# A planned order with corrected costs, and constant products ahead of planned TensorE waits

## The chip, the cores and the metric

The kernel runs on one core of one Trainium2 chip. A core has engines that run side by side: TensorE (PE; its weight loads are listed as PEld), VectorE (DVE), ScalarE (ACT), GpSimd (POOL) and SyncE (SP), which here issues nearly all DMA transfers. The metric is the device time of one launch in microseconds (us), lower is better. A profile is one execution recorded by the hardware profiler.

## The reference, cut to what matters

The input is 32 images of 56 x 56 pixels with 96 channels. Each goes through a conditional convolution block, a frequency-domain mixing layer and a quantised feed-forward layer:

```python
pooled = mean(x, (1, 2)); rw = sigmoid(pooled @ Wr + br)            # 4 expert weights per image
h = relu(bn1(x @ sum_e rw[e] * Wpw[e] + rw @ bpw))                   # 96 -> 384
h = relu(bn2(sum_e rw[e] * (depthwise3x3(h, Wdw[e]) + bdw[e])))
x = bn3(h @ sum_e rw[e] * Wpwl[e] + rw @ bpwl) + x                   # 384 -> 96

t = tokens(x)                                                        # 3136 x 96
h = relu(bn(layernorm(t) @ w1.T))                                    # 96 -> 192
X = fft(h, over tokens); xr, xi = relu(complex diagonal of X + bias)
t = t + bn(real(ifft(xr + 1j * xi)) @ w2.T)                          # 192 -> 96
u = relu(q(q8(layernorm(t)) @ q8(W1).T + b1))                        # 96 -> 384, q8: float8 e5m2
t = t + q(q8(u) @ q8(W2).T + b2)                                     # 384 -> 96, q: float16
```

## The kernel before, in words

After a preparation (constants, the transform matrices, the first image's loads) the whole run is recorded as a list of operations, image by image, by `record(b)` (line 767). Nothing is issued while it is recorded. An operation (`Op`, line 151) is one small piece of work on one engine: a group of matmuls, one copy out of PSUM, one DMA. It has a planned duration, a due time, the buffers that it reads, writes and takes, and a function that emits its instructions.

`Plan.order()` (line 269) then plays the list through as a small event simulation. Each engine starts, among the operations whose inputs are done and whose buffers are free, the one with the earliest due time. The due time is set from the table `WANT` (when in the image's period a stage should run), plus `NUDGE`, one number per operation of an image (572 of them, sought beforehand by an automatic search), minus `HURRY` for the DVE and ACT operations that read PSUM, so that they go first. An operation's input counts as ready after a lag per engine, and for a DMA after its modelled landing (`DMA_LAG`, `packets`), plus the reader's `slack`: 2.0 us for a DMA that `move` (line 231) records, unless it is given, and none for `add` (line 236). Buffers come from rings; PSUM is one ring of eight banks (`Banks`, line 97), from which an operation takes one, two or four when it starts, and to which they are given back when the last reader is done. At the end (lines 1477 and 1478) the operations are emitted in the order in which the simulation started them, and `Pinned` (line 370) keeps that order in the program. On the chip, each engine works its instructions off in this order; semaphores make it wait where an operand or a place is not there yet.

The stages of an image, with the names that the profile shows:

- `pad` (line 787, ACT) copies the loaded image into a padded layout and sums it; `spread` and a small matmul (`ps<-wr_s,pooled`) give the four expert weights; `mixed` (line 831, DVE) mixes the weights.
- The expansion (`ps<-x,wk`). Of six groups of 128 channels, three get their depthwise convolution from VectorE (`by_vector`, 869) and three from TensorE (`by_tensor`, 928): DMAs regroup the channels (`hp<-h`), `conv` (line 976) runs 128 small matmuls `ps<-hp,wg`, and DMAs bring the result back (`h<-hp`). `project` (1030) is `ps<-h,wk` and `ps<-h,wkc`.
- `moments` (1075) transposes strips of the image (`ps<-ident,x`) and takes their mean and variance, with a power function on POOL (`root`); `hidden` is `ps<-w1c,x`; `along_h` (1161) is the transform along h (`ps<-ha,da`), stored to DRAM as gd.
- The frequency stage, in seven groups of four or five frequencies: a load `g2`, `along_q` (1215, `ps<-dftb_s,g`; its first group also has `ps<-ones,nsa`), element-wise work on ACT and DVE (tiles za, zb, tmpa, tmpb), `second` (1288, `ps<-w2b,zb` and `ps<-w2a,za`), `back_q` (`ps<-zo,dftc_s`), stored to DRAM as yd.
- The last stage, in four strips: loads `yt`, `dd`, `xs`; `back_h` (1361, `ps<-dd,yt`) transforms back, DVE adds into xs, `moments` again (`ps<-ident,xs`), `normal` on ACT, `turn_back` (1397, `ps<-ident,nt`), `up` (1416, `ps<-n,fw`, three times), ReLU on ACT, a cast on POOL, `down` (1442, `ps<-h,fw`, three times), the addition on POOL and the store. The tile `h16` between `up` and the cast has two places.

Operations of up to three images are under way at once, so that one image's last stage runs beside the next one's convolutions.

Of the kernel before, what the change touches and what calls it, by code (L numbers as in the profile page):

```python
# [18 lines left out]
NE = 4  # L19
C = 96  # L20
M = 384
# [7 lines left out]
PB = 2 * S  # L29
# [48 lines left out]
class Ring:  # L78


    def __init__(self, places):
        self.places = places
        self.rest = 0.0
        self.free = list(range(len(places)))
# [8 lines left out]
    def give(self, got):  # L93
        self.free.extend(got)

# [55 lines left out]
class Op:  # L151
    __slots__ = ("eng", "dur", "due", "emit", "bufs", "takes", "left", "ready", "after", "end", "seq", "size", "slack", "port")
# [12 lines left out]
def packets(n, size):  # L165
# [7 lines left out]
WANT = dict(period=113.9, half=60.1, expand=0.0, vector=1.4, forward=10.7, forward_step=27.0, freq=172.2,  # L173
            freq_step=7.0, tail=259.2, tail_step=26.5, x=17.0, mix=33.5, project=33.0)

HURRY = 666.0
# [6 lines left out]
    -172.8, -9.2, -163.5, -60.3, 106.2, -144.5, 5.2, 53.2, -138.8, -8.2, -18.1, 99.5, 147.5, 94.2, 30.4, 67.4, 92.4, -148.5,  # L183
    -6.5, -38.5, 17.2, -12.9, -15.4, -66.7, 8, 47.3, 43.1, -21, 54, 5.1, 79, 62.9, 70.9, 46, 65.8, 61.6,
    84.4, 85, 84.4, 40.6, -2.1, 87.1, 20.9, 22, 0.2, 78.2, 60.5, 28.6, 19, 81.3, 37.6, 57.2, 88.1, 56.4,
    66.3, 27.8, 87.7, 47.1, 3.9, -118.2, -64.2, -84.3, -87, 1.7, 38, -13.3, 3.3, 79.4, -68.9, 6.1, -39.3, -22.4,
    -19.6, 33.1, 71.9, 22.4, 90.3, 8.3, 105.6, -2.6, 53.5, -90.3, -62.6, -103.8, -44.5, 28.1, 84, 81.8, 41.1, 65.4,
    8.5, -38.6, -23.9, -6.9, 6.4, 31.1, 20.5, -24.2, -49.9, -25.7, -1.2, 35.9, 4.4, 29.3, 35.4, 31.7, 11.2, 32.7,
    -0.6, 2.9, 64.3, 55.4, 21.5, 6, 26.4, -13.2, -2.6, -11, -7.5, -46.8, -15.5, -65, -6.8, -1.4, -9.5, -61.2,
    -31.8, -58.5, 20.3, 11.2, -20.3, -4.1, -1.5, -38.9, -22.4, 22.3, 23.7, -10.1, 25.5, 18, -0.4, 34.1, 24.9, 15.9,  # L190
    16.3, -10.2, 31.4, 20, 22.3, 21.4, 68.6, 6.5, 20.6, 32.1, 45.3, 0.2, 87.8, 97.5, 26.2, 165.3, 25.8, 69.2,
    -2.3, 75.7, -13.1, 128.9, -49.1, -108.2, -48.2, -13.1, 8.1, -3, 25.2, 64.8, 93.3, -26.5, -18, -36.1, -44, 25,
    40.1, 17.9, -68.7, -67.4, -63.8, -83.2, 48.6, -63, 51.9, -62.9, 51.9, 52.1, -44.3, -24.4, -95.9, 11.6, 10.1, -125.8,
    -87.7, -2.9, -83.3, 1.2, -12.6, -52.9, -15.4, 74.6, -82.7, 30.3, -7, 42.3, 39.1, -114.4, 9.2, -95.3, 27.5, 21,
    -15.1, 18.2, 13.7, -47.5, 10, 15.9, -62.4, -63.7, 18.7, -75.9, 1.4, -102.1, 66, 13.6, -89.4, -47.9, -79.5, 7.9,
    27.8, -78.8, -48.7, -13.9, -80.9, 7.2, -17, -75.7, 2.9, 34.7, -79.6, 18.7, -29.5, -51.1, 29.1, -120.2, -27, -174.8,
    -19.6, -1.7, -101.7, -132.1, -25.7, -135.5, -3.1, -29.4, -68.3, -35, -106.8, -36.1, -32.9, -24.2, -19.8, -72.9, -51.2, -26.6,
    -193.3, -161, -26, -32.5, -13, -23, 2, -38.4, -26.7, -48.1, -139.2, -94.1, -29.8, -21.3, -65.4, -22.5, -55.3, -54.9,
    -104, 2.6, 50, -62.3, -1.2, -99.1, -50, -31.3, -93.3, -124, -30.2, 30.5, -6.3, -48.4, 9.1, -63.1, 23.9, -32.4,
    -123.4, -98.1, -13.4, -29.5, 2.9, -15.5, -54.1, -85.5, -81.5, -70, -65.3, -64.4, -9.9, -63.4, -67.9, -49.2, -238.5, -138.2,  # L200
    -51.4, -18.7, -39.4, -87.4, -30.3, -73.9, -33.3, -80.2, -229.8, -126.4, -52, -64, -103.4, -40.4, -65.3, -50.3, -83.5, -2.5,
    -2.7, -75.9, -43, -126.9, -9.5, -24.2, -129.6, -23.3, 4.8, 37.3, 44.5, 14.3, 64.3, -80.5, 24.6, -6, -141, -113.4,
    -0.5, -18.6, 6.6, -17.9, -90.6, -142.3, -89.1, -9.7, 39.2, 0.3, 64.2, -29.5, 14.3, 27.4, -160.3, -34.4, 20.7, 9.1,
    18.6, 19.1, 34, -87.3, 22.2, -20.8, -79.3, -114.3, -21, -1.7, -46.5, 1.5, -56.6, -68.3, -96, -11.4, 7.3, -31,
    -1, -113.3, -20.1, -2.5, -133.2, -104.9, -6.8, 32.5, -0.9, 15.3, 67.8, -62.8, 32.2, -0.4, -84, -89.1, 48.2, -11,
    9.3, 43.2, -1.5, -48, -40.4, 3.9, 40.7, -28.9, 46.7, -47.5, 12.9, 24.6, -140.4, -106.2, 23.3, 13.5, -12.4, 27.8,
    13.9, -47.3, -7.4, 5.3, -87, -93, 11.7, 18.1, -83.2, -13.4, -87, -74.7, 14.1, 53.6, 39.4, 15.6, -33.3, 7,
    -90, -14.5, -32.6, -58, -68.1, -127.6, 70.6, -91.1, -82, -120.2, -128, -95.6, -46.5, -198.2, -126.4, -74.2, -83.7, -138.5,
    -99, -84.9, -60.2, -28.1, 23.8, -92.6, 27.3, -29.5, -3, 14.7, 11.8, 22.6, 27.2, -37.4, -126.3, -32, -88.4, -49.7,
    -80.9, -115.3, 44.8, -36.2, -64.3, -126.9, -78.2, -25.2, -36.4, -46, -79, -23.3, -32.1, -93.1, -97.6, -15.3, -44.1, 7.2,  # L210
    69.9, -69, -43.9, 51.1, 2.7, 75.7, 49.8, 54.4, 62.2, -32.2, -53.4, 7.7, -51.1, -6.4, 24.5, -84.8, 136.4, -14.6,
    6.6, -88.3, -65, 0.9, -18.3, -70.5, -45.5, 2.6, -12.9, -65.1, -65.4, -0.1, -18.6, -23.2, 77.8, -37.1, 0.8, -7.6,
    5, 67.2, 25.4, 103.6, 150.3, 33.5, -55.5, 40.7, -47.9, 2.3, 49.7, -3.5, 176, 13.2, -18.2, -66.6, -65.7, -28.6,
    15.8, -58.1, 11, 16.7, -29, -88, -20.9, 33.5, -35.4, 17.5, 44.4, -13.1, 48.4, 59.1,
# [4 lines left out]
class Plan:  # L219
# [16 lines left out]
    def add(self, eng, dur, due, emit, reads=(), writes=(), takes=(), size=0, port=None):  # L236
        op = Op()
# [5 lines left out]
        op.takes, op.size, op.slack = list(takes), size, 0.0  # L243
# [25 lines left out]
    def order(self):  # L269
# [19 lines left out]
        def start(op, now):  # L289
            for b in op.takes:  # L290
                b.got = b.ring.take(b.n)
            begin = now
# [41 lines left out]
        while events:  # L334
            now = events[0][0]
            while events and events[0][0] <= now:
# [11 lines left out]
                elif kind == "give":  # L348
                    for b in x.bufs:
                        b.users -= 1  # L350
                        if b.users == 0:
                            if b.ring.rest:
                                push(now + b.ring.rest, "back", b)
                            else:
                                b.ring.give(b.got)
                else:
                    x.ring.give(x.got)
# [28 lines left out]
def kernel(  # L386
# [380 lines left out]
    def record(b):  # L767
# [7 lines left out]
        for st in range(NS):  # L775
# [11 lines left out]
            def pad(st=st, h=h, k=k, sx=sx):  # L787
# [8 lines left out]
                takes=[mix, *xh] if st == 0 else [],  # L796
# [39 lines left out]
        def mix_wk2():  # L836
# [8 lines left out]
            "DVE", 3.08, t0 - WANT["mix"], lambda: mixed(wk.ap, wpw_s, wpw_s[:, NE], C + 1), port=True,  # L845
# [82 lines left out]
        def by_tensor(h, c, due, hid):  # L928
# [47 lines left out]
            def conv():  # L976
# [13 lines left out]
                "PE", 3.8, due, conv, reads=[(wg, 0), *((hp, r) for r in range(4))],  # L990
# [84 lines left out]
        def moments(p, of, key, due, out_extra):  # L1075
# [30 lines left out]
            add("POOL", 1.78, due + 1, root, port=False, writes=[(ln, 0)])  # L1106
# [3 lines left out]
        for st in range(NS):  # L1110
# [22 lines left out]
            for q0, nq in ((0, 4), (4, 3)):  # L1133
# [27 lines left out]
                def along_h(q0=q0, nq=nq, ps=ps, ha=ha, da=da):  # L1161
# [11 lines left out]
                    "PE", 0.82, due + 3, along_h, reads=[(ha, 0), (da, 0)], writes=[(ps, 0)], takes=[ps, g],  # L1173
# [24 lines left out]
        for i, (k0, nk) in enumerate(GROUPS):  # L1198
# [7 lines left out]
                reads=gd_parts, writes=[(g2, 0)], takes=[g2],  # L1206
# [268 lines left out]
    for b in range(NB):  # L1475
        record(b)
    for op in plan.order():
        op.emit()
# [114 lines left out]
```

## Time and profile before

| what | value |
|---|---|
| median of 3 runs | 4395.16 us (4389.32 to 4395.35) |
| profiled execution, its own time | 4390.8 us |
| its span, first to last instruction | 4389.0 us |
| mean granted TensorE clock | 0.95 |
| TensorE busy | 3988.9 us (91%) in 40066 matmuls |
| VectorE, ScalarE, GpSimd busy | 3551.2, 3110.9 and 1632.2 us |
| DMA | 679.25 MB, mean 155 GB/s |
| chain of work that ended last | PE 46%, ACT 19%, DVE 13%, DMA 9%, POOL 6% |

A line of the profile names the engine, the operation, what it writes and reads by the program's tile names without their numbers, the shapes, and a count. Where every operation goes through one helper, all have that helper's line (L380), so one reads by names. In brackets or behind the last bar stands the time that the engine stood idle before the instruction, and what ended it; where several operands were awaited, the one that came last by the profile is named. "issue" means that nothing in the profile was awaited. A busy time of PE is the union of its matmuls from start to modelled end.

### The profile page before, as it was taken

What the parts mean: (1) busy time and instruction counts of PE and PEld (TensorE: products, weight loads), DVE (VectorE), ACT (ScalarE), POOL (GpSimd) and SP (SyncE); (2) the same over time, 40 slices, a digit from 0 to 9 for tenths busy, and PEclk for the clock granted to TensorE, in tenths of its full rate; (3) what the DMA queues carried; (4) which work ended last, traced back from release to release, by engine and by line L of the source; (5) the groups of instructions that cost most, each with busy time, mean ns of one, the idle gap of its engine ahead of it and who ended that gap; (6) DMA issues with size and microseconds to landing.
All of it is one profiled execution on the core that took longest, in us unless ns stands there. A gap on an engine that the chain in (4) does not pass through costs nothing.

```text
span 4389.0 us, 104599 instructions
## 1 busy us (share of the span) xinstructions
PE 3988.9 (91%) x40066; PEld 2522.6 (57%) x40066; DVE 3551.2 (81%) x9036; ACT 3110.9 (71%) x6281; POOL 1632.2 (37%) x1332
## 2 busy tenths in 40 slices
PE   2888999999999999999999999999999999999985
PEld 0455655666565665655666655566565566665663
DVE  5877777798888889877888888888977888888853
ACT  1456766677777777766778777777876777877765
POOL 1223333333334434333333434433433333343333
PEclk9988999999999999999999999999999999999986
DMA  5754776666776666676666777666667666667642
GB/s 119 139 140 118 168 162 144 154 147 170 172 169 164 162 161 160 164 160 149 154 154 154 174 175 168 167 161 152 162 162 162 159 156 149 162 170 178 157 130 65
DMA packets 427749, 679.25 MB, mean 155 GB/s; under 512 B 155062, under 2 KB 290678, under 8 KB 427206
## 3 DMA queue, kind: packets, MB, share of 16 engines
q1 hardware_dynamic: 421632, 668.08, 64.8%
q8 instruction: 316, 5.18, 0.5%
q10 hardware_dynamic: 5618, 4.49, 0.4%
q14 instruction: 183, 1.50, 0.1%
HBM read 300.21 MB, written 211.04 MB: 116 GB/s over the span
## 4 chain that ended last, share of the span: by engine, by line
PE 46%; ACT 19%; DVE 13%; DMA 9%; POOL 6%; issue 4%; SPq 1%; POOLq 0%; ACTq 0%; DVEq 0%
PE ps L380 46%; ACT h L380 6%; ACT nt L380 5%; POOL ln L380 5%; DVE ln L380 3%; DVE ha L380 3%; ACT tmpa L380 2%; DMA hp<-h 2%; DMA yt<-yd 2%; DMA da<-dad 2%; DVE za L380 2%; DVE tmpa L380 2%; DVE h L380 1%; ACT tmpb L380 1%; ACT y L380 1%
## 5 line engine op out<-in xcount | busy, mean ns | idle before, releaser
L380 DVE SCALAR_TENSOR_TENSOR h<-h,small,h 128x784 f32<-128x784 f32 x1536 | 1557.0, 1050 | 103.3 <-ACT h L380 84.5
L380 POOL CAST h<-h 128x784 fp8e5<-128x784 f16 x384 | 511.2, 1335 | 738.3 <-ACT h L380 738.3
L380 PE MATMUL ps<-x,wk 97*32 97x435 f32 (+2 forms) x3840 | 698.7, 571 | 9.3 <-DVE wk L380 9.1
L380 POOL TENSOR_TENSOR ln<-ln,mhalf 120x7 f32<-120x7 f32 (+1 forms) x256 | 473.9, 1851 | 21.3
L380 PE MATMUL ps<-hp,wg 32*32 32x392 f32 x12288 | 420.4, 520 | 48.6 <-DMA hp<-h 28.1
L380 POOL TENSOR_SCALAR ln<-ln 120x7 f32<-120x7 f32 (+1 forms) x256 | 130.0, 508 | 866.4 <-DVE ln L380 866.4
L380 PE MATMUL ps<-dftb_s,g 112*128 112x112 f32 (+1 forms) x3776 | 432.1, 288 | 12.5 <-DVE tmpa L380 9.9
L380 ACT ACTIVATE h<-ps 128x435 f32<-128x435 f32 (+2 forms) x768 | 388.7, 543 | 69.8 <-PE ps L380 55.6
L380 PEld LDWEIGHTS ps<-dftb_s,g 112*128 112x128 f32 (+1 forms) x3776 | 353.3, 172 | 143.9 <-issue 41.9
L380 DVE SCALAR_TENSOR_TENSOR ha<-ps,ln,nshift 120x192 f32<-120x192 f32 x896 | 306.4, 408 | 155.7 <-PE ps L380 150.3
L380 DVE BATCH_NORM_STATS2 ln<-ps 120x6 f32<-120x96 f32 (+1 forms) x1792 | 315.8, 247 | 69.2 <-PE ps L380 68.5
L380 PEld LDWEIGHTS ps<-x,wk 97*32 97x32 f32 (+1 forms) x3840 | 203.6, 125 | 276.1 <-issue 141.9
L380 ACT ACTIVATE h<-h,fb 128x784 f16<-128x784 f16 x384 | 361.1, 965 | 1.3
L380 PEld LDWEIGHTS ps<-hp,wg 32*32 32x32 f32 x12288 | 218.7, 105 | 232.0 <-issue 106.9
L380 PE MATMUL ps<-w1c,x 96*120 96x192 f32 x1792 | 342.7, 342 | 6.6 <-issue 5.5
L380 ACT ACTIVATE nt<-ps,ln 112x96 fp8e5<-112x96 f32 x896 | 301.7, 436 | 62.6 <-DVE ln L380 58.7
L380 PEld LDWEIGHTS <-fw 96*128 96x128 fp8e5 (+1 forms) x1536 | 155.5, 115 | 315.7 <-issue 214.6
L380 ACT CAST h<-ps 128x784 f16<-128x784 f32 x384 | 308.7, 828 | 36.0 <-PE ps L380 34.5
L380 ACT ACTIVATE hp<-ps,small 128x392 f32<-128x392 f32 x384 | 202.1, 598 | 178.2 <-PE ps L380 163.0
L380 PEld LDWEIGHTS ps<-w1c,x 96*120 96x120 f32 x1792 | 301.7, 189 | 45.8 <-issue 29.8
L380 POOL TENSOR_TENSOR xs<-xs,y 96x784 f32<-96x784 f32 x128 | 238.1, 1860 | 238.6 <-DVE y L380 238.6
L380 PE MATMUL ps<-h,wk 32*96 32x392 f32 x3072 | 316.2, 496 | 2.8 <-DMA h<-hp 1.0
(171 smaller groups left out, 7313.0 us busy)
## 6 DMA issues: line engine op xcount, KB each, us to landing
hp<-h SPq DMA_DIRECT2D x384, 217.5 KB
h<-hp SPq DMA_DIRECT2D x384, 196.0 KB
gd<-g SPq DMA_DIRECT2D x384, 192.0 KB
g<-gd SPq DMA_DIRECT2D x192, 336.0 KB
dd<-ddd SPq DMA_DIRECT2D x128, 392.0 KB
yt<-yd SPq DMA_DIRECT2D x128, 336.0 KB
xd<-park SPq DMA_DIRECT2D x128, 294.0 KB
xs<-xd SPq DMA_DIRECT2D x128, 294.0 KB
```

Source lines behind the costliest of these rows:

```text
L380: return self.tc.keep_in_program_order(method(*args, **kwargs))
```

## The change

The change has three parts.

- Durations in the plan are changed to others: the weight mix, `conv`, `root`, `along_h`, `second`, `back_h`, `normal`, `turn_back`, `up` and the cast. Three readers of DMA data or DRAM stores get another slack: `pad` 2.5 us (before 0), the `g2` load 3.5 (before 2.0), `back_h` 4.0 (before 0).
- All 572 numbers of `NUDGE` are replaced, `HURRY` goes from 666.0 to 1060.2 and the period from 113.9 to 114.0. The order of the operations on each engine changes with them.
- When the simulation starts an operation it notes how long its engine and the places that it takes had already been free (`op.wait`): what is left is a wait for data. Ahead of each TensorE operation that takes PSUM banks and whose planned wait is over 0.76 us, `int((wait - 0.5) / 0.26)` matmuls of two constants (`ident8` and `fw1`, float8, 96 rows, 112 x 384) are emitted. They write the first of the operation's own banks, which it then overwrites.

The diff, with the 572 numbers left out:

```diff
@@ class Ring
         self.rest = 0.0
+        self.since = {}
...
+    def given(self, got, now):
+        self.give(got)
+        for k in got:
+            self.since[k] = now
@@
-WANT = dict(period=113.9, half=60.1, expand=0.0, vector=1.4, forward=10.7, forward_step=27.0, freq=172.2,
+WANT = dict(period=114.0, half=60.1, expand=0.0, vector=1.4, forward=10.7, forward_step=27.0, freq=172.2,
...
-HURRY = 666.0
+WARM = 0.26
+
+HURRY = 1060.2
...
 NUDGE = [
...
@@ Plan
-    def add(self, eng, dur, due, emit, reads=(), writes=(), takes=(), size=0, port=None):
+    def add(self, eng, dur, due, emit, reads=(), writes=(), takes=(), size=0, port=None, slack=0.0):
...
-        op.takes, op.size, op.slack = list(takes), size, 0.0
+        op.takes, op.size, op.slack = list(takes), size, slack
@@ Plan.order
         def start(op, now):
+            clear = 0.0
             for b in op.takes:
                 b.got = b.ring.take(b.n)
+                clear = max(clear, *(b.ring.since.get(k, 0.0) for k in b.got))
+            op.wait = now - max(free[op.eng], clear)
...
-                                b.ring.give(b.got)
+                                b.ring.given(b.got, now)
                 else:
-                    x.ring.give(x.got)
+                    x.ring.given(x.got, now)
@@ record
                 "ACT", 0.84, t0 - WANT["mix"] - 10 + 2 * st, pad, reads=[(sx, 0)], writes=[(xh[h], k), (mix, ("sum", st))],
-                takes=[mix, *xh] if st == 0 else [],
+                takes=[mix, *xh] if st == 0 else [], slack=2.5,
...
-            "DVE", 3.08, t0 - WANT["mix"], lambda: mixed(wk.ap, wpw_s, wpw_s[:, NE], C + 1), port=True,
+            "DVE", 2.57, t0 - WANT["mix"], lambda: mixed(wk.ap, wpw_s, wpw_s[:, NE], C + 1), port=True,
...
-                "PE", 3.8, due, conv, reads=[(wg, 0), *((hp, r) for r in range(4))],
+                "PE", 3.75, due, conv, reads=[(wg, 0), *((hp, r) for r in range(4))],
...
-            add("POOL", 1.78, due + 1, root, port=False, writes=[(ln, 0)])
+            add("POOL", 1.95, due + 1, root, port=False, writes=[(ln, 0)])
...
-                    "PE", 0.82, due + 3, along_h, reads=[(ha, 0), (da, 0)], writes=[(ps, 0)], takes=[ps, g],
+                    "PE", 0.81, due + 3, along_h, reads=[(ha, 0), (da, 0)], writes=[(ps, 0)], takes=[ps, g],
...
-                reads=gd_parts, writes=[(g2, 0)], takes=[g2],
+                reads=gd_parts, writes=[(g2, 0)], takes=[g2], slack=3.5,
...
-                "PE", 0.29 * nk + 0.1, due + 5, second, reads=[(zs[0], 0), (zs[0], 1), (zs[1], 0), (zs[1], 1)],
+                "PE", 0.47 * nk - 0.45, due + 5, second, reads=[(zs[0], 0), (zs[0], 1), (zs[1], 0), (zs[1], 1)],
...
-            add("PE", 1.43, due, back_h, reads=[(yt, 0), (dd, 0)], writes=[(ps, 0)], takes=[ps])
+            add("PE", 1.44, due, back_h, reads=[(yt, 0), (dd, 0)], writes=[(ps, 0)], takes=[ps], slack=4.0)
...
-            add("ACT", 2.1, due + 4, normal, reads=[(ps, 0), (ln, 0)], writes=[(nt, 0)], takes=[nt])
+            add("ACT", 2.22, due + 4, normal, reads=[(ps, 0), (ln, 0)], writes=[(nt, 0)], takes=[nt])
...
-            add("PE", 0.55, due + 5, turn_back, reads=[(nt, 0)], writes=[(ps, 0)], takes=[ps, n8])
+            add("PE", 0.4, due + 5, turn_back, reads=[(nt, 0)], writes=[(ps, 0)], takes=[ps, n8])
...
-                add("PE", 0.4, due + 7, up, reads=[(n8, 0)], writes=[(ps, 0)], takes=[ps, h16])
+                add("PE", 0.36, due + 7, up, reads=[(n8, 0)], writes=[(ps, 0)], takes=[ps, h16])
...
-                    "POOL", 0.79, due + 9.5,
+                    "POOL", 0.82, due + 9.5,
@@ end of the kernel
+    def warm(op):
+
+        for buf in op.takes:
+            if op.eng == "PE" and buf.ring is banks and op.wait > WARM + 0.5:
+                for _ in range(int((op.wait - 0.5) / WARM)):
+                    te.matmul(buf.bank()[:PB, 0:M], ident8[:C], fw1, start=True, stop=True)
+
     for op in plan.order():
+        warm(op)
         op.emit()
```

## The prediction

> **What bounds the kernel now.** I read the page first: its busy line, the row of the granted clock and the DMA queues.
>
> ```profile
> span 4389.0 us, 104599 instructions
> PE 3988.9 (91%) x40066; PEld 2522.6 (57%) x40066; DVE 3551.2 (81%) x9036; ACT 3110.9 (71%) x6281; POOL 1632.2 (37%) x1332
> ...
> PEclk9988999999999999999999999999999999999986
> ...
> q8 instruction: 316, 5.18, 0.5%
> ```
>
> TensorE (PE) is the bound, and its clock is under full speed in nearly every slice. Next, busy time by stage: the start, the 29 images whose routing matmul (`ps<-wr_s,pooled`, one per image) lies between 252.8 and 4042.6 us, the end; then the quickest image, a slow one, and two short stretches.
>
> ```profile
> 0.00:77.50 77.50, 0.95 (x2) 0.40 (x3) 39.99 (x174) 7.00 (x17) 14.46 (x22) 1.00 0.46 122
> 77.50:252.80 175.30, 145.77 (x1548) 78.53 (x1548) 138.99 (x261) 81.46 (x153) 38.98 (x28) 0.86 0.66 129
> 252.80:4042.60 3789.80, 3562.57 (x36221) 2255.31 (x36218) 3164.78 (x7987) 2790.74 (x5646) 1459.54 (x1174) 0.96 0.68 160
> 4042.60:4389.00 346.40, 279.63 (x2301) 188.34 (x2299) 207.49 (x617) 231.75 (x468) 119.19 (x109) 0.83 0.46 120
> 2366.10:2491.70 125.60, 118.96 (x1255) 75.10 (x1254) 109.34 (x278) 96.70 (x197) 50.51 (x41) 1.00 0.70 167
> 1823.30:1962.80 139.50, 129.54 (x1254) 82.26 (x1253) 109.83 (x278) 96.84 (x198) 50.98 (x41) 0.93 0.65 150
> 1805.60:1809.00 3.40, 2.16 (x16) 1.16 (x16) 2.11 (x5) 3.24 (x8) 0.00 (x0) 1.00 0.96 185
> 1809.00:1815.80 6.80, 6.80 (x39) 6.11 (x40) 5.29 (x20) 5.07 (x11) 3.29 (x3) 0.50 0.55 152
> ```
>
> After the length stand PE, PEld, DVE, ACT and POOL busy, then the clock. An image takes 3789.8/29 = 130.7 us, the quickest 125.6 at clock 1.00, the slow one 139.5 at 0.93. The last two lines show the mechanism: one 3.4 us stretch with 2.16 us of PE work, then half clock for 6.8 us. The clock records hold 48 such spells between 400 and 4160 us, 242 us in all, nearly all full of work that takes twice as long (the `ps<-dd,yt` matmuls follow each other at 187 instead of 96 ns): a loss of about 121 us. By the window before them, 14 spells follow a wait of `ps<-dd,yt` (61 us, loss 31), 23 the start of the frequency stage (116 us, loss 58), 7 a stop in or just behind the grouped convolution (51 us, loss 26), 4 its data (14 us, loss 7).
>
> What PE waits for between 400 and 4160 us, by group:
>
> ```profile
> L380 PE MATMUL ps<-hp,wg 32*32 32x392 f32 x11136 | 378.8, 518 | 37.5 <-issue 19.6 <-DMA hp<-h 17.8
> ...
> L380 PE MATMUL ps<-dd,yt 116*96 116x112 f32 x1603 | 214.2, 296 | 66.7 <-ACT zo L380 27.7 <-issue 17.2 <-DMA yt<-yd 14.0
> ...
> L380 PE MATMUL ps<-n,fw 96*128 96x392 fp8e5 x694 | 176.5, 335 | 53.8 <-ACT h L380 34.0 <-DVE tmpa L380 11.2 <-ACT n L380 5.2
> ...
> L380 PE MATMUL ps<-h,fw 128*96 128x392 fp8e5 x690 | 165.2, 341 | 30.1 <-ACT h L380 22.8 <-DVE tmpa L380 6.7 <-POOL h L380 0.3
> ```
>
> The column behind the second bar is idle time. `dd,yt` (the inverse transform along h) waits longest, 66.7 us. Last, one slow place in order of time:
>
> ```profile
> 1884.58 0.87 PE L380 MATMUL ps<-h,fw 128*96 128x392 fp8e5 x4 [0.63 <-ACT h L380]
> 1887.17 2.53 PE L380 MATMUL ps<-dd,yt 116*96 116x112 f32 x14 [1.72 <-DMA yt<-yd]
> 1889.49 0.86 PE L380 MATMUL ps<-h,fw 128*96 128x392 fp8e5 x2
> 1890.28 3.81 PE L380 MATMUL ps<-hp,wg 32*32 32x392 f32 x106
> 1897.36 1.25 PE L380 MATMUL ps<-hp,wg 32*32 32x392 f32 x22 [3.27 <-issue]
> ```
>
> PE waits 1.72 us for yt, falls to half clock, then stops for 3.27 us inside one convolution, where no operand is missing. The packet records of queue q8 explain that stop: 316 packets of 16 KB for some 81,000 PE instructions is one per 256; nine such stops, here and in the `w1c` matmuls behind, stand at the same remainder of the instruction count and end 1.25 to 1.63 us after a packet. PE ran out of instructions. An image has 2534 of them, 230 beyond a multiple of 256, so the place shifts by 26 per image and returns after about ten: the slow images come in runs near 650, 1900 and 3300 us.
>
> **The change part by part.** The sum goes against the profiled execution, 4390.8 us (span 4389.0); the median shown, 4395.16, is 0.1% above it.
>
> *The wait of `back_h`.* The plan now holds yt and dd ready 4.0 us after their landing as it models it, before at once. Work that is ready goes ahead of `back_h`, which removes waits up to 4.0 us; the longest in this stretch is 3.04. Of the 66.7 us, 17.2 is "issue", beside which I count nothing. Of the other 49.5 I take four fifths, **-40**; the rest stays because the filled work must exist. Late next: the DVE addition into xs, the moments and the feed-forward part behind it, at most 4 us later in a chain that spans several stages. Bounds: 0 (something else is waited for) to -67.
>
> *The clock after it.* 14 spells, loss 31: two thirds, **-20**; bounds 0 and -31.
>
> *Costs and order.* The corrected costs agree with rows: weight mix 4 x 0.62 = 2.5 us (plan 3.08, now 2.57), `turn_back` 0.34 to 0.40 between starts (0.55, now 0.40), `up` 0.34 (0.40, now 0.36). `second` goes from 1.26 to 1.43 for four groups; the rows give 0.56 + 0.86 to 0.94 between starts, so that too is right. None runs faster for it; only the order shifts. HURRY 1060.2 for 666.0 puts readers of PSUM further ahead, and `n,fw` with `h,fw` wait 83.9 us, mostly for ACT's copy out of PSUM and its ReLU. With the 58 us of clock at the start of the frequency stage, 142 us is at stake. The trace of before shows no new order: bounds -142 and, since an order can also meet DMAs worse, +66, a second `dd,yt` wait. I take **-20**, nearer to nothing, since most of this wait has a place as its cause, not data. The other two slacks cost nothing by themselves: on ACT, `pad` now follows copies that are ready, and the routing behind it has the 10 us that it is due ahead; on SP the `g2` load goes later among DMAs, where the queue waits 450 us for ACT's `y` and 334 for `g` anyway, and behind it stand the next stores of gd and yd.
>
> *The constant products.* Price from the `n,fw` pair, same type and 392 columns: 0.34 us for two with their weight loads, 0.17 each at full clock, twice that at half. They stand where the planned data wait is over 0.76 us, (wait - 0.5)/0.26 of them, so at full clock they fill about two thirds of what is over 0.5. A wait for a bank or an SBUF place gets none, and `n,fw` waits for just that. Each waits for the bank that the operation behind it needs in any case, so a free bank means no new wait. In a real wait they cost nothing; a wait of 1.7 us gets four, 0.7 us, and the window above would rise from 2.16 to some 2.8 of 3.4, at the edge (windows with 2.6 to 2.8 still led to spells). Saving **-5**, bounds 0 and -26. Where the planned wait is not there each costs 0.17: two per image, **+10**; bounds 0 and 30 per image, +150. Ahead of the first routing matmul they cost nothing: `fw1` is cast at 32.1 us, PE idles from 47.7 to 77.5. At the end, 116 us run at half clock from 4168 on and PE has 38% of the chain there; products could return some 15 of the 38 us lost: **-12** for all of it, bounds 0 and -20.
>
> On the clock, the Trainium skill, page "TensorE: Matmul & The Clock Gate", section "Why this matters for your kernels", says a drop to half rate takes a TensorE gap of over about 3 us between bursts. The rows disagree: the stretch at 1805.6 has gaps of 0.90 and 0.34 us. By the page the clock terms and the products' saving would be nought and the sum -40 - 12 + 10 = -42.
>
> *Unchanged:* the stops for instructions (19.6 + 5.5 us and loss 26) and the convolution's data (17.8, loss 7), as no cost of theirs is altered: 0.
>
> Sum: -40 - 20 - 20 - 5 + 10 - 12 = -87; 4390.8 - 87 = 4304. Rounded up, since whatever is moved ahead makes something else late: 4310.
>
> **The rivals.** *All images like the best.* 29 x (130.7 - 125.6) = 148, with the end 160: **4230**. For: nothing in an image's work needs more. Against: instructions still run out.
>
> *Only the waits count.* If small gaps don't set the clock, 40 for `dd,yt`, 12 for the order's waits (84/142 of 20) and the price of the products are left: 4390.8 - 40 - 12 + 10 = **4349**. Against: in only 6 of the 48 windows is there a gap of 3 us.
>
> *No change.* The late yt is replaced by the next late landing, hp or a place of h16, at the same length: **4390**.
>
> *Slower: instructions run out in every image.* Each product adds two instructions. Thirteen per image make 2560, exactly ten packets; then the place no longer shifts, and if it stands in the convolution every image is a slow one. The twelve slow images average 135.6 us: 29 x (135.6 - 130.7) = +142, less 87, **4446**. It decides from 87/142 of that, when the slow images rise from 12 in 29 to about 22. For: a denser PE asks for packets faster. Against: the remainder is as likely harmless.
>
> *Slower: products where nothing is waited for.* With slack 4.0 the plan may see waits of 3 us ahead of `back_h` that are 0.5 us in the trace. Without its product term the sum is -97, gone at 18 such products an image (32 x 18 x 0.17 = 98); at 25 it is 136 - 97 = +39: **4430**. Against: the plan's order was sought so that PE waits little.
>
> **How the numbers follow.** The likeliest, 4310 (own range 4270 to 4350), 0.42; the best images 0.16; only waits 0.05; no change 0.09; instructions 0.13; products 0.10; an order that meets the DMAs worse, up to +66, 0.05. Faster by over 0.2% (8.8 us, about what a measurement can tell) 0.63, within 0.09, slower 0.28. Signs of both kinds are held by the cases, so the range goes from 4215, a little under 4230, to 4450, just over 4446: what is left out is the worse half of the slow cases and little below.
>
> **What would show it.** Right: idle before `dd,yt` under 30 us, fewer spells of half clock (under 35 between 400 and 4160), images at 128 us. Wrong: "issue" waits of PE over 60 us; a new group `ps<-ident,fw` with over 18 products an image and PE busy time grown by more than 60 us; idle before `hp,wg` or `n,fw` grown by what `dd,yt` lost.

## The result, and the profile after

The changed kernel takes 4326.5 us, the median of four runs (4312.69 to 4341.59), where the kernel before, measured beside it, takes 4392.24: a ratio of 0.985, with a 95% interval of 0.982 to 0.989. The forecast was 4310. The profiled execution took 4312.69 us, 78.1 less than that of before, and its span is 4309.7 us, 79.3 less. It is the quickest of the four, 13.8 us under their median, so what follows shows a little more than the medians' 65.7 us.

The page of the changed kernel, the lines that answer to those of before: busy time, granted clock, the instruction queue, and the chain that ended last.

```profile
span 4309.7 us, 105146 instructions
PE 3902.5 (91%) x40391; PEld 2482.1 (58%) x40391; DVE 3613.7 (84%) x9036; ACT 3079.6 (71%) x6281; POOL 1657.3 (38%) x1332
...
PEclk8999899999999999999999999999999999999997
...
q8 instruction: 318, 5.21, 0.6%
...
PE 38%; DVE 28%; ACT 17%; DMA 9%; issue 5%; SPq 1%; POOL 1%; POOLq 0%; DVEq 0%; ACTq 0%
```

PE is busy for 86.4 us less, although it runs 325 matmuls more (the products). Its share of the chain fell from 46 to 38%, and that of DVE rose from 13 to 28%: where PE waits now, it waits more often for DVE. By stage, with the columns as before (length; PE, PEld, DVE, ACT and POOL busy; clock; DMA):

```profile
77.50:251.50 174.00, 162.84 (x1722) 92.00 (x1723) 149.53 (x288) 87.91 (x170) 39.17 (x28) 0.90 0.69 140
251.50:3971.70 3720.20, 3435.82 (x36247) 2181.79 (x36246) 3228.53 (x8005) 2767.09 (x5669) 1486.19 (x1177) 0.97 0.70 163
3971.70:4309.70 338.00, 292.26 (x2374) 200.00 (x2374) 195.64 (x571) 217.48 (x430) 117.47 (x105) 0.87 0.45 116
```

The 29 images between the routing matmuls take 3720.2 us instead of 3789.8, 128.3 each instead of 130.7. That is 69.6 of the 79.3 us; the end gives 8.4, the start 1.3. I split the middle into three: idle time of PE; the clock loss, which is half of the PE work done while the clock records show half clock; and the rest, PE's busy time net of that loss.

| middle, us | before | after | difference |
|---|---|---|---|
| PE idle | 227.2 | 284.4 | +57 |
| clock loss (half-clock spells) | 129.3 (50) | 113.6 (44) | -16 |
| PE busy, net of clock loss | 3433.3 | 3322.2 | -111 |

So PE waits longer in the open, and the gain stands in its busy time. First, four groups of before between 400 and 4160 us:

```profile
L380 PE MATMUL ps<-ha,da 56*64 56x192 f32 x3712 | 234.1, 339 | 3.6 <-DVE ha L380 0.4 <-issue 0.2
...
L380 PE MATMUL ps<-w2b,zb 64*112 64x96 f32 x1658 | 132.4, 276 | 0.0
...
L380 PE MATMUL ps<-ident,nt 112*96 112x112 fp8e5 x812 | 59.9, 214 | 1.8 <-DVE ha L380 0.4
...
L380 PE MATMUL ps<-wr_s,pooled 96*128 96x4 f32 x56 | 9.5, 240 | 0.0
```

Then the groups of the changed kernel between 400 and 4100 us:

```profile
L391 PE MATMUL ps<-hp,wg 32*32 32x392 f32 x11136 | 349.4, 520 | 16.8 <-issue 16.6
...
L391 PE MATMUL ps<-ha,da 56*64 56x192 f32 x3680 | 187.6, 333 | 3.9 <-issue 0.8
L391 PE MATMUL ps<-dd,yt 116*96 116x112 f32 x1624 | 185.6, 267 | 25.0 <-DMA yt<-yd 19.2 <-issue 3.3 <-DVE ln L391 2.0
L391 PE MATMUL ps<-n,fw 96*128 96x392 fp8e5 x692 | 178.3, 355 | 30.1 <-ACT h L391 25.2 <-DVE ha L391 4.9
...
L391 PE MATMUL ps<-h,fw 128*96 128x392 fp8e5 x690 | 166.1, 351 | 28.9 <-ACT h L391 11.1 <-ACT nt L391 10.8 <-POOL h L391 6.8
...
L391 PE MATMUL ps<-w2b,zb 64*112 64x96 f32 x1664 | 134.5, 278 | 92.9 <-DVE zb L391 62.5 <-ACT g L391 24.8 <-DVE mix L391 3.7
...
L391 PE MATMUL ps<-ident,nt 112*96 112x112 fp8e5 x805 | 61.3, 216 | 25.9 <-ACT y L391 25.1 <-ACT zo L391 0.7
...
L391 PE MATMUL ps<-wr_s,pooled 96*128 96x4 f32 x56 | 10.8, 263 | 29.3 <-ACT y L391 28.9 <-DVE tmpb L391 0.3
...
L391 PE MATMUL ps<-fw,ident 96*112 96x384 fp8e5 x1 | 0.3, 326 | 0.0
```

The wait of `dd,yt` went from 66.7 to 25.0, that of `hp,wg` from 37.5 to 16.8 (its share for data from 17.8 to none), that of `n,fw` from 53.8 to 30.1. In their place stand waits that before did not have: `w2b,zb`, the first matmuls of `second`, waits 92.9 us (before 0.0), 62.5 of them for DVE's `zb` and 24.8 until ACT has copied `g` out of PSUM; the routing matmul 29.3 (before 0.0) and `ident,nt` 25.9 (before 1.8) for ACT's `y`. The last line is the products: **one** in this whole stretch. Of the 325, 110 stand ahead of 251.5 us and 214 behind the last routing matmul.

Where does busy time go, if the matmuls are the same? One place of it can be read in the timeline (start, length, operation). First before, then after, in images at full clock:

```profile
2413.01 3.43 PE L380 MATMUL ps<-h,wk 32*96 32x392 f32 x32
2416.37 0.94 PE L380 MATMUL ps<-h,wkc 128*96 128x392 f32 x2
```

```profile
2336.31 2.89 PE L391 MATMUL ps<-h,wk 32*96 32x392 f32 x32
2339.13 1.30 PE L391 MATMUL ps<-h,wkc 128*96 128x392 f32 x3
```

The same 32 matmuls take 3.36 us from start to the next operation before, and 2.82 after. Over the middle's images at full clock the means are 3312 and 2819 ns, and 6498 and 5453 ns for the 64 matmuls of the other half: 1.54 us per image, **45 us** over 29. These matmuls run in four groups of rows side by side, each group into a bank of its own. After, the first matmuls of the groups start 0, 6, 13 and 20 ns after the first. In the operation of before shown here they start at 0, 6, 135 and 557 ns: the third and the fourth wait for ACT's semaphore, which was set 42 and 43 ns ahead of their start. Over the middle of before 101 of these matmuls start within 80 ns of such a semaphore, set as ACT ends an operation that empties a bank (`h<-ps` 54 times, `nt<-ps,ln` 47 times); after, 4 do. While one group works PE counts as busy, so this lateness appears in no idle column (there `ps<-h,wk` has 1.6 us in before). It is a wait inside busy time.

The rest lies elsewhere. Clear of half clock and without idle time, PE's busy time per image falls by 1.5 us in `ps<-h,wk`, 1.4 in `ps<-ha,da`, 1.0 in `ps<-hp,wg` and 0.6 in `ps<-x,wk`, and rises by 0.4 in `ps<-h,fw`. All groups together fall by 4.1 us, 118 over 29 images. What was late in `ps<-ha,da` and the others was not separated.

### The profile page after: what moved, and what is told of

It is laid out like the page before. It is cut to its first block, busy times and chain, and to the rows that moved or that the text cites. A ratio compares the mean times of both kernels' runs of the same rounds, so it can differ in the third digit from the quotient of the medians.

```text
span 4309.7 us, 105146 instructions
## 1 busy us (share of the span) xinstructions
PE 3902.5 (91%) x40391; PEld 2482.1 (58%) x40391; DVE 3613.7 (84%) x9036; ACT 3079.6 (71%) x6281; POOL 1657.3 (38%) x1332
## 4 chain that ended last, share of the span: by engine, by line
PE 38%; DVE 28%; ACT 17%; DMA 9%; issue 5%; SPq 1%; POOL 1%; POOLq 0%; DVEq 0%; ACTq 0%
PE ps L391 38%; DVE h L391 9%; DVE ln L391 5%; ACT nt L391 5%; DMA yt<-yd 4%; ACT h L391 4%; DMA yd<-y 3%; DVE ha L391 3%; DVE za L391 3%; DVE zb L391 2%; DVE tmpb L391 2%; DVE wk L391 2%; ACT tmpa L391 2%; DVE tmpa L391 1%; SPq L391 1%
## 5 line engine op out<-in xcount | busy, mean ns | idle before, releaser
L391 POOL CAST h<-h 128x784 fp8e5<-128x784 f16 x384 | 585.3, 1528 | 1436.8 <-ACT h L391 1436.7
L391 PE MATMUL ps<-dftb_s,g 112*64 112x112 f32 (+1 forms) x3776 | 435.3, 288 | 18.3 <-DVE ln L391 14.0
L391 PEld LDWEIGHTS ps<-dftb_s,g 112*64 112x64 f32 (+1 forms) x3776 | 354.4, 173 | 128.9 <-issue 61.7
L391 POOL TENSOR_TENSOR ln<-ln,mhalf 120x7 f32<-120x7 f32 (+1 forms) x256 | 419.2, 1637 | 21.3
L391 DVE BATCH_NORM_STATS2 ln<-ps 112x6 f32<-112x96 f32 (+1 forms) x1792 | 318.5, 250 | 115.3 <-PE ps L391 115.1
L391 PE MATMUL ps<-hp,wg 32*32 32x392 f32 x12288 | 388.1, 521 | 21.6 <-issue 16.6
L391 POOL TENSOR_TENSOR xs<-xs,y 96x784 f32<-96x784 f32 x128 | 274.0, 2140 | 259.1 <-DVE y L391 256.1
L391 ACT ACTIVATE h<-h 128x784 f32<-128x784 f32 x192 | 164.0, 856 | 176.5 <-DVE h L391 174.8
L391 PE MATMUL ps<-h,wkc 128*96 128x392 f32 x768 | 284.9, 519 | 0.0
```

What stands on the lines that cost most here:

```text
L391: return self.tc.keep_in_program_order(method(*args, **kwargs))
```

## The experiments

Four questions: which part of the change gains; whether the old order with the one late landing would have done it; what the place of the instructions is worth; and what products are worth where PE really waits. None of these kernels leaves out any of the computation; some add constant matmuls whose result is overwritten.

**The order without products.**

```diff
-    def warm(op):
...
-        warm(op)
```

> The changed kernel without its constant products; order, costs and slacks stay. Theory (the gain is the order's: the profile after has 325 products, of which 110 stand in the first 252 us, 214 behind the last routing matmul, and one between): 4325 to 4340 us, at most 12 more than with them, and between 252 and 3972 us the same waits. Rival (the products carry the gain): 4360 us or more.

Measured: 4318.6 us (4313.4 to 4333.6), ratio 0.983 [0.981, 0.986]. The interval overlaps that of the full change. In the middle 40 spells of half clock instead of 44, 128.9 us per image instead of 128.3; the start is 6.3 us longer than with products (180.3 for 174.0) and the end 18 shorter (320.1 for 338.0). PE's busy time net of clock loss is 3323.2 us in the middle, as good as with products (3322.2). The whole gain is there without the products, those of the end included.

**The products without the order:** the old numbers, costs, slacks, HURRY and period, with the rule for products.

```diff
+            op.wait = now - max(free[op.eng], clear)
...
+        warm(op)
```

> The old numbers, costs, slacks and HURRY with the rule for the products added. Theory: products again only at the start and the end, 4375 to 4392 us, the middle as before. Rival (products keep the clock up): 4340 us or less and fewer than 35 spells of half clock in the middle.

Measured: 4390.1 us, ratio 0.999 [0.997, 1.000]. 250 products, three of them in the middle. They change nothing that can be measured.

**The new costs and slacks with the old numbers.**

```diff
-            "DVE", 3.08, t0 - WANT["mix"], lambda: mixed(wk.ap, wpw_s, wpw_s[:, NE], C + 1), port=True,
+            "DVE", 2.57, t0 - WANT["mix"], lambda: mixed(wk.ap, wpw_s, wpw_s[:, NE], C + 1), port=True,
...
-            add("PE", 1.43, due, back_h, reads=[(yt, 0), (dd, 0)], writes=[(ps, 0)], takes=[ps])
+            add("PE", 1.44, due, back_h, reads=[(yt, 0), (dd, 0)], writes=[(ps, 0)], takes=[ps], slack=4.0)
```

> The kernel before with the new durations and all three slacks, but the old 572 numbers and the old HURRY. Theory (numbers and costs belong together, so an order not sought for these costs is no better): 4380 to 4480 us, with less idle before dd,yt and more elsewhere. Rival (correct costs alone give the better order): 4340 us or less.

Measured: 4873.4 us, ratio 1.110 [1.107, 1.112]. The images fall into groups of three, some 110, 183 and 138 us long. The middle grew by 439 us, of which 260 idle and 212 clock, in 113 spells. That it would be no better was expected, the size was not: the costs are closer to the trace, and the old numbers with them give a far worse order.

**Only the late yt.**

```diff
-            add("PE", 1.43, due, back_h, reads=[(yt, 0), (dd, 0)], writes=[(ps, 0)], takes=[ps])
+            add("PE", 1.43, due, back_h, reads=[(yt, 0), (dd, 0)], writes=[(ps, 0)], takes=[ps], slack=4.0)
```

> The kernel before with the slack of 4.0 us on back_h alone. By the prediction's first step the idle time before dd,yt falls from 66.7 to under 30 us and the time by 40 to 60 us, to some 4335. Rival (the wait goes elsewhere): dd,yt falls all the same, but other groups wait as much more and the time is 4375 to 4450 us.

Measured: 4681.6 us, ratio 1.066 [1.063, 1.068]. Both expectations were far off. The groups of this run between 400 and 4000 us:

```profile
L380 PE MATMUL ps<-dd,yt 116*96 116x112 f32 x1428 | 177.2, 280 | 13.1 <-ACT zo L380 4.8 <-DVE ln L380 3.4 <-ACT hp L380 2.5
L380 PE MATMUL ps<-n,fw 96*128 96x392 fp8e5 x614 | 160.9, 350 | 81.2 <-ACT h L380 55.2 <-ACT n L380 15.0 <-DVE ha L380 2.4
L380 PE MATMUL ps<-w2b,zb 64*112 64x96 f32 x1476 | 135.6, 301 | 35.6 <-ACT y L380 12.1 <-DVE zb L380 10.2 <-DVE ha L380 4.0
...
L380 PE MATMUL ps<-ident,xs 96*112 96x96 f32 x714 | 84.0, 261 | 28.7 <-DVE xs L380 28.1 <-issue 0.4 <-DVE tmpb L380 0.2
```

The wait that the slack aims at is gone (13.1, and nothing for yt among what is named), as it should be. What follows it is late instead: `ident,xs` waits 28.7 us for the addition into xs, `n,fw` 81.2, `w2b,zb` 35.6. The middle is 260 us longer, of which 181 idle and 119 clock. The slack does its work in the place that it names, and by itself costs 284 us.

**The new numbers with the old costs.**

```diff
-            "DVE", 2.57, t0 - WANT["mix"], lambda: mixed(wk.ap, wpw_s, wpw_s[:, NE], C + 1), port=True,
+            "DVE", 3.08, t0 - WANT["mix"], lambda: mixed(wk.ap, wpw_s, wpw_s[:, NE], C + 1), port=True,
...
-            add("PE", 1.44, due, back_h, reads=[(yt, 0), (dd, 0)], writes=[(ps, 0)], takes=[ps], slack=4.0)
+            add("PE", 1.44, due, back_h, reads=[(yt, 0), (dd, 0)], writes=[(ps, 0)], takes=[ps])
```

> The changed kernel with the old durations and slacks under the new 572 numbers, the new HURRY and period. Theory (numbers fit only the costs that they were sought for): 4500 to 4900 us, as the old numbers with the new costs took 4873. Rival (the numbers alone carry the gain): 4340 us or less.

Measured, in one run: 4795.3 us, images of 105 to 236 us. The rule for products puts 442 of them into this plan, 167 in the middle; at 0.19 us each (worked out below) that is some 30 us of the 400. Numbers and costs belong to each other; neither half of the change carries the gain.

**The place of the instructions.** 16 products per image bring 2529 instructions to 2561, one over ten packets, so an image keeps its place in the packets almost unchanged. `fixed_wide` has them 384 columns wide, `fixed_narrow` 8 wide, and `fixed_wide_shift` is `fixed_wide` with 64 more ahead of the first image, where PE waits anyway: the same work, 128 instructions further on. In the diff the first `extra` is that of the routing matmul (for the shift, `4 + (64 if b == 0 else 0)`), the second that of `second`.

```diff
+    def constant(op):
+        for _ in range(op.extra):
+            te.matmul(op.takes[0].bank()[:PB, 0:384], ident8[:C], fw1[:, 0:384], start=True, stop=True)
...
-        )
+        ).extra = 4
...
-            )
+            ).extra = {3: 5, 5: 7}.get(i, 0)
```

> The changed kernel with 16 more constant products in every image where its trace has PE waiting for data: 4 ahead of the routing matmul (wait 1.07 us), 5 and 7 ahead of second in the fourth and the sixth group of frequencies (0.92 and up to 1.59 us). Theory (PE's work in a window of 3.4 us sets the clock): the spells of half clock in the middle fall from 44 to under 28, and the loss by them from 114 to under 80 us; 4280 to 4300 us. Rival (only gaps of over 3 us cost the clock): 40 spells or more, 4320 to 4345 us.

> The same 16 products with 8 columns in place of 384: the same instructions at the same places of the program, with hardly any work. Theory: as many spells as in the changed kernel (38 to 48), and 25 to 45 us more than with the wide ones, with the stops for instructions at the same images. Rival (only gaps of over 3 us cost the clock): the same time as with the wide ones within 10 us.

> The wide products, and 64 more ahead of the first image's routing matmul, where PE idles for 30 us: all later TensorE instructions stand 128 places further on. An image has some 2561 instructions then, ten packets of 256 and one, so the place of a packet's end hardly moves from image to image. Theory (PE stops where a packet ends inside the grouped convolution behind dd,yt): of this kernel and the one without the 64, one has such stops in over 15 images and the other in under 5, and they differ by 40 us or more. Rival (the stops come from DMA traffic, whatever the place): both have 5 to 12, and the times lie within 15 us.

Measured: `fixed_wide` 4263.4 us, ratio 0.972 [0.969, 0.974]; `fixed_narrow` 4287.7, 0.977 [0.975, 0.979]; `fixed_wide_shift` 4482.2, 1.022 [1.019, 1.025]. The groups between 400 and 4000 us, of `fixed_wide` and then of `fixed_wide_shift`:

```profile
L392 PE MATMUL ps<-hp,wg 32*32 32x392 f32 x11008 | 345.9, 512 | 1.6 <-issue 1.5
L392 PE MATMUL ps<-dd,yt 116*96 116x112 f32 x1596 | 174.8, 261 | 12.4 <-DVE ln L392 6.3 <-DMA yt<-yd 6.1
...
L392 PE MATMUL ps<-fw,ident 96*112 96x384 fp8e5 x449 | 86.8, 325 | 29.5 <-ACT y L392 29.2 <-DVE tmpb L392 0.3
```

```profile
L392 PE MATMUL ps<-hp,wg 32*32 32x392 f32 x10368 | 345.9, 532 | 61.4 <-issue 61.4
L392 PE MATMUL ps<-dd,yt 116*96 116x112 f32 x1512 | 177.4, 268 | 51.3 <-issue 33.1 <-DMA yt<-yd 18.0 <-DVE ln L392 0.2
```

`fixed_wide` came out below the 4280 to 4300 that were expected. It has 19 spells in the middle, with 51 us lost by them; `fixed_narrow` has 27, with 94 us, where 38 to 48 spells were expected, and takes 24 us more. So the work of the products keeps the clock up, though by a little less than expected, and the same instructions with hardly any work already bring 39 us (4326.5 to 4287.7).

The waits named "issue" go from 1.5 to 61.4 and from none to 33.1 us, and one convolution in order of time, in `fixed_wide_shift`, shows the two stops:

```profile
2024.67 0.64 PE L392 MATMUL ps<-dd,yt 116*96 116x112 f32 x5 [1.26 <-issue]
2025.15 0.76 PE L392 MATMUL ps<-h,fw 128*96 128x392 fp8e5 x2
2025.84 4.88 PE L392 MATMUL ps<-hp,wg 32*32 32x392 f32 x120
2032.16 0.86 PE L392 MATMUL ps<-hp,wg 32*32 32x392 f32 x8 [1.44 <-issue]
```

By the packet records of q8, 29 stops of over 1 us lie inside `hp,wg`, nearly one per image, at the same remainder of the instruction count (193 or 194 beyond a multiple of 256), and end 1.2 to 1.7 us after a packet. `ps<-dd,yt` ahead of it has 21 more at this remainder. Before and after have 10 stops of over 1 us each at this remainder, in the convolution and the matmuls around it, and `fixed_wide` one. Moving the place by 128 instructions costs **219 us**. In the profiled executions the middle is 204 us longer: idle time 124 (93 of them in the two waits named "issue"), clock loss 69 and other busy time 10. The product ahead of the routing matmul also shows that a product cannot fill a wait for a place: the first one stands behind the 29.2 us wait for ACT's `y` that the routing matmul had.

**The old order, held in place.** The kernel before, with 13 tiny products per image ahead of `back_h` (2560 instructions), and 16 ahead of the first image to put the packet's end away from the convolution, or 97 in the same line to put it there.

```diff
+            te.matmul(op.takes[0].bank()[0:32, 0:8], ident8[:C, 0:32], fw1[:, 0:8], start=True, stop=True)
...
-        )
+        ).extra = 16 if b == 0 else 0
...
-            add("PE", 1.43, due, back_h, reads=[(yt, 0), (dd, 0)], writes=[(ps, 0)], takes=[ps])
+            add("PE", 1.43, due, back_h, reads=[(yt, 0), (dd, 0)], writes=[(ps, 0)], takes=[ps]).extra = (4, 3, 3, 3)[st]
```

> The kernel before, with 13 tiny constant products per image (32 x 8 outputs) ahead of back_h, 4 in the first strip and 3 in the others, so that an image has 2560 TensorE instructions, ten packets, and 16 more ahead of the first routing matmul, so that the routing matmuls stand some 150 behind a multiple of 256, where the quick images of its own trace stood (146 to 172). Theory (its slow images are those in which a packet ends inside the grouped convolution): no stop there, every image at 126 to 128 us, 4265 to 4300 us, so the old order would be as quick as the new one in the same place (4288 with narrow products). Rival (the new order is better in itself): no stops either, but 4320 to 4360 us.

> The same with 97 products at the start for 16: the routing matmuls stand some 56 behind a multiple of 256, where the slow images stood (68, 42). Theory: a stop in nearly every image, 135 to 139 us an image, 4480 to 4600 us. Rival (the stops come from DMA traffic): a third of the images at most, 4400 us or less.

Measured: apart 4339.7 us, ratio 0.988 [0.985, 0.990], with no stop for instructions; within 4435.8, ratio 1.009 [1.006, 1.012], with only six stops of over 1 us, but longer waits for yt (40.2 us in the stretch instead of 16.2). For the second neither time came true, as its place mostly avoided the convolution. In the first, what had been expected of an old order as good as the new one, 4265 to 4300, did not come: held in place, the old order takes 4339.7 and the new one, with as many instructions and narrow products, 4287.7. So the rival came true, and the 52 us between are the order's own, as far as the different places of the tiny products allow. In the middle of the profiled executions the new order has 81 us more idle time, 44 less clock loss and 87 less of other busy time. The products of `old_held_apart` also show what one wait of `back_h` is:

```profile
L381 PE MATMUL ps<-fw,ident 96*32 96x8 fp8e5 x364 | 26.4, 170 | 27.2 <-ACT zo L381 27.2
```

The wait for ACT's `zo`, 27.7 us ahead of `dd,yt` before, stands ahead of the products here. They read constants alone and write a bank, so it is a wait for a bank. The run also says what held instructions are worth to the kernel before: 4392.2 - 4339.7 = 53 us.

**Products in one place where PE waits for data.** The longest wait of `second` in the changed kernel stands in the sixth of the seven groups (index 5), 1.59 us in some 20 of the 29 images. `one_place` puts 6 wide and 10 tiny products there; `one_place_tiny` has `(0, 16)` there, 16 tiny ones, so that the number and place of the instructions are the same.

```diff
-            )
+            ).extra = (6, 10) if i == 5 else (0, 0)
```

> The changed kernel with 16 products per image at one place, ahead of second in the sixth group, where PE waits 1.59 us for DVE: 6 of 384 columns and 10 tiny ones (32 x 8). In fixed_wide the 4 ahead of the routing matmul stood behind the same wait of 1.07 us as before (it is for a bank) and the 5 ahead of the fourth group behind 0.18 us, so those nine cost 1.5 us an image. Theory (work in the window sets the clock, the held place ends the stops, and products in a wait cost nothing): no stops, no spell behind this wait, 4225 to 4250 us. Rival (the nine were what kept the clock up): spells back over 30, 4270 us or more.

> The same with 16 tiny products and no wide one: the same instructions at the same place without the work. Theory: no stops either, the spells behind the wait are back, 15 to 40 us more than with six wide ones. Rival (only gaps of over 3 us cost the clock): within 8 us of it.

Measured: 4233.3 us (4228.5 to 4241.2), ratio 0.964 [0.961, 0.966], and 4277.7, ratio 0.975 [0.972, 0.978]. The place in order of time, in `one_place` and then in `one_place_tiny`:

```profile
2270.84 0.81 PE L392 MATMUL ps<-zo,dftc_s 112*112 112x384 f32 x2
2271.48 1.48 PE L392 MATMUL ps<-fw,ident 96*112 96x384 fp8e5 x16
2273.24 0.64 PE L392 MATMUL ps<-w2b,zb 64*112 64x96 f32 x8 [0.28 <-DVE zb L392]
```

```profile
2293.40 0.81 PE L392 MATMUL ps<-zo,dftc_s 112*112 112x384 f32 x2
2294.14 0.55 PE L392 MATMUL ps<-fw,ident 96*32 96x8 fp8e5 x16
2295.80 0.64 PE L392 MATMUL ps<-w2b,zb 64*112 64x96 f32 x8 [1.10 <-DVE zb L392]
```

In both `second` begins 2.40 us after the start of the `zo,dftc_s` pair ahead of it (2.41 in the changed kernel, without products); with the wide products PE works for most of it. The middle is 31 us shorter with them in the profiled executions (3635.9 for 3666.6): 63 us less clock loss (31.8 in 11 spells for 94.7 in 37), 32 us more work, idle time the same within 1 us. Between the medians it is 44 us, a little over the 15 to 40 that were expected. `one_place` is the fastest kernel of the study, faster than both: 0.964 / 0.985 = 0.98 of the changed one.

## Why the prediction was right or wrong

The time, 4310 for 4326.5, came out within its own range (4270 to 4350), and so did an image's 128 us and the wait of `dd,yt` under 30 us. Of the terms of the sum the first two held in size, though the first is made up otherwise than was said. The order's, the three of the products and the nought for what was called unchanged did not hold, so that the sum came near by luck.

**The wait of `back_h`: -40 expected, -42 in the two traces** (66.7 to 25.0). The size is right, its make-up is not. The 17.2 us named "issue", beside which the step counted nothing, are waits for a landing: each of the eight ends 91 ns after a DMA landing whose semaphore PE had waited for just before, as do the 13 waits (7.9 us) named "DVE ln". With the 14.0 named yt, landings made up 39.1 us of before, and 21.2 after (19.2 and 2.0): 18 went. Another 27.7 went with the wait for ACT's `zo`, which is for a bank, and 3.3 us of stops for instructions came. Nor can this edit be priced alone: in the old order the same slack takes the wait away and costs 284 us. The step said that what is ready goes ahead and that the addition into xs and what follows is "at most 4 us later". That is where it failed as a price: `late_yt_alone` shows this lateness come back as a wait of `ident,xs`, of `n,fw` and of `second`. The numbers of the order had to be other ones, and in the change they are.

**The clock after it: -20.** I counted the spells between 400 us and the end of the middle again, each put to the longest gap that reaches into the 3.4 us window ahead of it, in both traces by the same rule. Ahead of 400 us, where this count begins, lie 12 of the 16 us of clock loss that the middle gave back.

| behind a gap before | spells, loss us: before | after |
|---|---|---|
| `n,fw` | 23, 57.4 | 5, 14.9 |
| `hp,wg` | 10, 30.2 | 4, 8.2 |
| `dd,yt` | 14, 28.5 | 3, 5.0 |
| `w2b,zb` | 0 | 20, 50.8 |
| `ident,nt` | 0 | 5, 18.2 |
| routing | 0 | 5, 8.5 |
| others | 1, 1.7 | 2, 9.2 |
| all | 48, 117.8 | 44, 114.8 |

Behind `dd,yt` 23.5 us went, as expected. Almost all of what the three old triggers gave back, 88 us, is lost again behind new ones. The prediction's sign for a right mechanism, fewer than 35 spells, did not come.

**Costs and order: -20 expected, the mis-sized term.** I had looked for its worth in the waits of `n,fw` and `h,fw` and in the clock behind `n,fw`. Those fell by 83.9 - 59.0 = 25 us and by 42. But the order also made new waits of PE, 146 us in `w2b,zb`, the routing matmul and `ident,nt`, with 78 us of clock behind them, and it took away 111 us of PE's busy time net of the clock loss, 45 of them shown above as lateness inside `ps<-h,wk`. None of this was in the prediction: it read waits from the idle column alone. Together the order gave -67 for the waits and the clock that the step had in view, -111 of busy time and +224 for the new waits with their clock: +46 where -20 stood. That the sum came near all the same is luck: the 43 us at `hp,wg`, which the prediction had at 0 (below), cancel most of the 66 us by which this term was off. `old_held_apart` beside `fixed_narrow` bears out that the new order is better by itself, by 52 us with the instructions held; `order_alone`, which leaves them to shift, is 79 us under before (4397.2 and 4318.6).

**The products: -5 + 10 - 12 expected, nothing measured.** `order_alone` is as fast as the changed kernel, and `products_alone` as the one before. The step assumed two per image; there was one in 29 images. What failed is the assumption that the plan sees the waits of the trace. It puts a product wherever it plans a data wait of over 0.76 us, so it planned none in the middle, save one, while the chip had 1.59 us ahead of `second` in most images. The price of a product (0.17 us at full clock) was nearly right: 6 wide ones and 10 tiny ones took 1.48 us, and 16 tiny ones 0.55; ten tiny ones are then some 0.34, which leaves 0.19 for a wide one. At the end they were to bring 12 us; without them the end is shorter by 18, in one profiled execution of each.

**Unchanged: 0 expected, -43 measured at `hp,wg`.** The count of stops for instructions stayed: 10 of over 1 us before, 10 after, though they are shorter (26.8 and 19.6 us together). An image has 2529 instructions instead of 2534, so the place shifts by 31 instead of 26 per image. But the wait of `hp,wg` fell by 21 us, 17.8 of them the wait for its data, and the clock loss behind it by 22. The step put these at nothing because no cost of theirs was altered; the order moved them all the same. Whether it brings the data earlier or asks for it later was not separated. The slower rival, 4446, needed ten whole packets per image; the change did not give them, but `fixed_wide_shift` built that case by hand and took 4482. Its mechanism is shown. The two times can't be compared, as 4446 also takes off 87 us for the other terms.

**The rivals.** "Only the waits count", 4349, is refuted for this kernel by `one_place_tiny`: the 16 tiny products leave the image's idle time as it is with wide ones and the time is 44 us longer. In the changed kernel, of 44 spells only three have a gap of 3 us or more in the window; 38 have none of 2 us. The windows and the clock of one such place, after:

```profile
2309.40:2312.80 3.40, 1.81 (x17) 1.18 (x16) 3.37 (x10) 1.99 (x5) 2.58 (x4) 1.00 0.22 55
2312.80:2316.20 3.40, 3.40 (x11) 1.52 (x10) 3.29 (x9) 2.66 (x5) 1.10 (x2) 0.50 0.00 1
```

```profile
2311.53 0.64 PE L391 MATMUL ps<-w2b,zb 64*112 64x96 f32 x8 [1.59 <-DVE zb L391]
```

A window with 1.81 us of work and one gap of 1.59 is followed by half clock. The Trainium skill, page "TensorE: Matmul & The Clock Gate", section "Why this matters for your kernels", puts the drop at a gap of over about 3 us; this trace doesn't agree with it. The same page's section "A second HAM failure mode: psum-queue depth-cycling" tells of a kernel whose short, frequent idle times made the clock swing, without a length for them; these rows show such a swing, behind one gap of 1.1 to 1.6 us in a window. "All images like the best", 4230, is what `one_place` reaches (4233.3), by the two causes that kept the changed kernel from it: spells behind one wait of `second` (44 us between it and `one_place_tiny`), and the place of the instructions (49 us between `one_place_tiny` and the changed kernel).

## What to carry to other kernels

Numbers that fit one set of a model's costs can give a far worse order with another set (4795.3 and 4873.4 us here): price such a change as a new order, not edit by edit, and expect new waits in the place of the old. Read waits also from start to start of the matmuls, since work in row groups hides lateness inside busy time. Put filler work where the trace of the finished kernel shows a data wait, not where the plan expects one, and count the instructions per loop before and after: a fixed number can hold a good place, or a bad one.

## What the runs showed of the hardware that was not expected

The place at which PE's packets of 256 instructions end is worth 219 us (4263.4 and 4482.2), 5% of the time, in programs that differ by 64 products at the start. The stop comes in the grouped convolution, where 128 matmuls with their 128 weight loads, one whole packet, take 3.66 to 3.70 us. The Trainium skill, page "Runtime: NRT & Kernel Launch", section "Instruction fetch mechanics", has the blocks of 256 instructions that q8's packets show, and calls the cost of crossing one mostly hidden. That holds for most of the packets here and not for the 29 stops.

A gap of 1.1 us can be enough to turn a 3.4 us window into one that half clock follows: in `one_place_tiny` the spells behind `second` have windows with 2.1 to 2.4 us of work, most of them around such a gap. It is not so each time. Laid on the grid of 3.41 us that the clock records of the changed kernel show, between 400 and 3900 us, none of 745 windows at full clock with less than 15% of idle time is followed by half clock, 13 of 152 with 15 to 35%, 23 of 54 with 35 to 50%, and all 6 with more. What decides between windows of the same idle time stays open. Six matmuls, some 1.1 us of work per image, put into one wait that they don't lengthen, take 26 of 37 spells away and 44 us off the time.
